# Reordering the border between the graph layers and the recurrence of a four-layer GNN kernel

## The chip, the cores and the metric

The kernel runs on one core of a Trainium2 chip. The metric is the device time of one execution in microseconds, as the median of several runs. The profile of one execution comes with it: its span, the instructions of each engine and the transfers. Engines are TensorE (PE; its weight loads are a row of their own, PEld), VectorE (DVE), ScalarE (ACT), GpSimd (POOL) and SyncE (SP), which here only issues transfers.

## The reference, cut to what matters

There are 16 graphs of 1024 nodes with 256 features. Each of four layers normalises x, applies relu, runs a graph operator and adds the result to x:

```
for layer in (attention, normalised adjacency, recurrence, MLP):
    h = relu(layernorm(x))
    x = x + layer(h, adj)
```

Layer 2 is the recurrence. With `dinv` the inverse row sums of `adj` (0 where a sum is 0), it goes through the nodes one after the other, and every node reads the states of its neighbours, new ones where they have been updated already:

```
norm_adjT = swapaxes(adj, 1, 2) * dinv[:, :, None]
for i in range(1024):                     # for all 16 graphs together
    x_par = norm_adjT[:, i] @ h           # sums over neighbours
    r, z  = split(x_i @ W_ioux.T + b_ioux + x_par @ W_iouh.T + b_iouh)
    r, z  = sigmoid(r), sigmoid(z)
    hc    = tanh(x_i @ W_coux.T + b_coux + (x_par * r) @ W_couh.T + b_couh)
    h[:, i] = z * x_par + (1 - z) * hc
```

## The kernel before, in words

**Layers 0 and 1** (`layers_0_1`) run as one loop over the graphs, i = 0 to 15. Matrix products with the adjacency are written as seven products of 512x512 quarters (`sums`, line 384), and the work of everything else is hung into seven hooks between these products: `a0` to `a6` in the first sums of an iteration (layer 0 of graph i), `d0` to `d6` in the second (layer 1 of graph i). In this part the order on all five engines, SyncE's queue included, is the order in which the Python code emits the instructions. `weights` (423) multiplies the sums by the layer's matrix; `Moments` (331) collects the layer norm's mean and variance, the squares on ScalarE; `normed` (361) applies relu((x - mean) * rs) on ScalarE, eight tiles of 128x256. The quarters lie in ten slots `at0` to `at9`.

**Jobs.** The recurrence wants its nodes in another order than the graph's (blocks of 128 nodes, inside a block 8 steps of 16, in an order that a side calculation finds on DVE). For every graph b a `Job` (497) brings what the recurrence reads into that order:

- `load` (513) gets `ad` (the adjacency near the diagonal, `near`, 1 MB), `ab` (the first block's columns, 0.5 MB) and, for b < 14, the normalised h, `h2`, from `he_d`. For 14 and 15 h2 stays where `normed` wrote it.
- `mask` (523) writes the permutation matrix `to` on DVE (L526) and zeroes triangles of `ad` and `ab` with affine selects on POOL (L529, L531); `scale` (534) multiplies `ad` by dinv on POOL, two instructions (L536, L537).
- `turn` (540) permutes and transposes h2 on TensorE (L547), evicts it (L550 ScalarE, L552 DVE) and stores it as `heT_d`.
- `first` (555) multiplies the first block's columns with h2 (L559), `base` (583) turns that into order and stores `base_d`.
- `order` (563) permutes `ad` (L570, L572), evicts it (L577 ScalarE, L579 DVE) and stores `near_d` and `next_d` (L580, L581).

Jobs 0 to 13 run two to an iteration, from i = 9 to 15, `run_a` in the first half and `run_b` in the second. Behind the loop stands a tail (from line 820): the rest of job 13, the last weights, and jobs 14 and 15 from their loads on.

**The border.** `layer_2` (866) begins with the weights `wx`, the biases, and small constants on DVE and POOL; then `load_he(0)` (1001) brings block 0 of `heT_d` for all graphs into `he`, in three parts (graphs 0 to 13, 14, 15); `Gates(he, 0)` (1040) copies the 16 columns of step 0 into `hs` on POOL (L1046) and multiplies them by `wx` on TensorE (L1056). `Sub(0, 0)` (1011) gathers 128 rows for each half of the graphs out of `near_d` into `aj` (L1020, indirect DMA on POOL) and spreads them into `ai` and `bd` on POOL (L1027, L1036). `bxt` is block 0's base, loaded from `base_d`; `wh` are the weights of the hidden state. In layer 2 the order on TensorE, DVE, ScalarE and POOL is that of the code; SyncE's queue is ordered by the scheduler, by when a load's slot is free.

**The recurrence** loops over 8 blocks t and 8 steps s. A step starts with x = bxt + near, runs `round_` (the gates of the hidden state, L1110), turns the new h and stores it; between its matmuls it works off a list of tasks: the gates of the next step, the far sums, and `base_tasks` (902), which compute the base of block t + 1 out of `ab` (columns) and `hb` (rows of he_d), one graph after another (L942). POOL masks each `ab` first (L920); ScalarE evicts each base sum (L929) ahead of the step's tanh. `last_tasks` (971) loads `ao` out of `next_d`, and `load_he(t + 1)` the next block's `he`. At the end of the recurrence layer 3 starts.

Of the kernel before, what the change touches and what calls it, by code (L numbers as in the profile page):

```python
# [16 lines left out]
P = 128  # L17
# [4 lines left out]
S = 16  # L22
# [20 lines left out]
def gnn_stack(ctx: ExitStack, tc: tile.TileContext, a: dict, out: bass.AP):  # L43
# [29 lines left out]
    dinv = const.tile([P, B, NT], F32, name="dinv")  # L73

# [194 lines left out]
    def layers_0_1():  # L269
        with ExitStack() as st:  # L270
# [226 lines left out]
            class Job:  # L497
# [24 lines left out]

                def mask(self):
                    b, ad, ab = self.b, self.ad, self.ab
                    self.to = to = self.tile("to", [P, NT, P])
                    nc.vector.tensor_tensor(to, step[:, None].to_broadcast([P, NT, P]),  # L526
                                            place.rearrange("i (t b) -> i t b", b=B)[:, :, b : b + 1].to_broadcast([P, NT, P]),
                                            ALU.is_equal)
                    nc.gpsimd.affine_select(out=ad[:, :, P:], in_=ad[:, :, P:], compare_op=ALU.is_gt, fill=0.0, base=0,  # L529
                                            pattern=[[0, NT], [-1, P]], channel_multiplier=1)  # L530
                    nc.gpsimd.affine_select(out=ab[:, 0], in_=ab[:, 0], compare_op=ALU.is_ge, fill=0.0, base=0,  # L531
                                            pattern=[[-1, P]], channel_multiplier=1)

                def scale(self):
                    b, ad = self.b, self.ad
                    nc.gpsimd.tensor_tensor(ad[:, :, P:], ad[:, :, P:], dinv[:, b][:, :, None].to_broadcast([P, NT, P]), ALU.mult)  # L536
                    nc.gpsimd.tensor_tensor(ad[:, 1:, :P], ad[:, 1:, :P],  # L537
                                            dinv[:, b, 1:][:, :, None].to_broadcast([P, NT - 1, P]), ALU.mult)

                def turn(self):  # L540
                    b, to = self.b, self.to
                    hT = big.tile([P, DC, N], F32, name=self.names.get("hT", "hT"))
                    for c in range(DC):
                        for t0 in range(0, NT, 4):
# [4 lines left out]
                            if t0 == 0 or not self.tail:  # L549
# [3 lines left out]
                    nc.gpsimd.dma_start(heT_d[b], hT)  # L553

                def first(self):
# [5 lines left out]
                    nc.scalar.activation(self.bs, pb[:, :D], AF.Copy, scale=dinv[:, b, 0:1])  # L561

                def order(self):
# [3 lines left out]
                    for t0 in range(0, NT, 2):  # L567
# [8 lines left out]
                        if t0 % 4 == 0:  # L576
                            nc.scalar.copy(got, pt)  # L577
                        else:
                            nc.vector.tensor_copy(got, pt)  # L579
                    nc.gpsimd.dma_start(near_d.rearrange("(t b j) n -> b j t n", t=NT, b=B)[b], ao[:, :, : P + S])  # L580
# [11 lines left out]
                def rest(self):  # L592
                    self.first()
                    self.order()
                    self.base()
# [49 lines left out]

            jobs = {i: (Job(2 * (i - 9)), Job(2 * (i - 9) + 1)) for i in range(9, 16)}
            jobs[15][1].names = {"ao": "h1"}
            job14 = Job(14, {"ad": "at7", "ab": "ds", "to": "at0", "hT": "q", "ao": "hT", "bs": "s1", "bo": "s2"})
            job15 = Job(15, {"hT": "h1", "ao": "q"})

            for i in range(B):
# [4 lines left out]
                def a0():  # L656
                    if ahead and i:
                        load_x(i + 1)
                    if run_a:
                        run_a.load()  # L660
                    side(1.0)
# [39 lines left out]
                def a6():  # L701
                    if ahead:
                        mean[i + 1].middle()
                        mean[i + 1].second(lo)
                    side(0.0 if run_a else 2.0)
# [40 lines left out]
                def d0():  # L746
                    if ahead:
                        plus(i + 1, "t1", "b11")
                        get(i + 1, "t3", 0, 1)
                    if m2:  # L750
# [8 lines left out]
                def d2():  # L759
# [4 lines left out]
                    if ahead:  # L764
                        add_f(i + 1, lo)
                    side(1.0)
# [6 lines left out]
                def d4():  # L773
# [5 lines left out]
                    if run_b:  # L779
                        run_b.mask()  # L780
                    side(0.5)
                def d5():
# [3 lines left out]
                    if run_b:  # L786
                        run_b.scale()
                def d6():
                    plus_row(x[i], "bias", 3)
                ags[i] = sums(i, left_of, [d0, d1, d2, d3, d4, d5, d6], lambda name: drop(i, name))  # L790
                if run_b and ahead:
                    run_b.turn()
                if m2:
                    m2.shift = small.tile([P, NT], F32, name="m_shift")
                    nc.vector.tensor_mul(m2.shift, m2.neg, m2.rs)
                if not ahead:
                    break
# [22 lines left out]
            h2[14] = big.tile([P, NT, D], F32, name="h2", bufs=2)  # L820
            normed(h2[14], x[14], m2.shift, m2.rs, all_)
            nc.sync.dma_start(rows(he_d[14]), h2[14])
            job14.load()
            m2 = Moments(x[15], "n", big.tile([P, 2, D], F32, name="s2").rearrange("p a d -> p (a d)")[:, :D])
            weights(x[15], ags[15], w1, dis[15], m2)
            nc.sync.dma_start(rows(x2_d[15]), x[15])
            m2.root()
            run_b.first()
            run_b.turn()
            shift = small.tile([P, NT], F32, name="shift")  # L830
            nc.vector.tensor_mul(shift, m2.neg, m2.rs)
            job14.mask()
            run_b.order()
            run_b.base()
            job14.scale()
            h2[15] = big.tile([P, NT, D], F32, name="h2", bufs=2)
            normed(h2[15], x[15], shift, m2.rs, all_)
            nc.sync.dma_start(rows(he_d[15]), h2[15])
            job15.load()
            job14.first()  # L840
            job14.turn()
            job14.base()
            job15.mask()
            job15.turn()
            job15.first()
            job15.base()
            job15.scale()
            job14.order()
# [17 lines left out]
    def layer_2(shared, early):  # L866
        with ExitStack() as st:
            wp = st.enter_context(tc.tile_pool(name="w2", bufs=1, reuse_waits="tile"))
# [7 lines left out]
            load_w(wx, "W_iouxT", "W_couxT")  # L876

            bias = wp.tile([P, 3, DC], F32, name="bias")
            bias2 = wp.tile([P, 3, DC], F32, name="bias2")
            with nc.allow_non_contiguous_dma(reason="biases, once"):  # L880
                for t, io, co in ((bias, "b_ioux", "b_coux"), (bias2, "b_iouh", "b_couh")):
                    nc.sync.dma_start(t[:, :2].rearrange("p q c -> p (q c)"), a[io].rearrange("(k p) -> p k", p=P))
                    nc.sync.dma_start(t[:, 2], a[co].rearrange("(c p) -> p c", p=P))
            nc.vector.tensor_add(bias, bias, bias2)
# [17 lines left out]
            def base_tasks(t, bxt):  # L902
# [4 lines left out]
                def load(b):  # L907
                    ab = big.tile([P, NT, P], F32, name="ab")
                    nc.sync.dma_start(ab, a["columns"][b, t])
                    hb = shared.tile([P, NT, D], F32, name="hb")  # L910
# [60 lines left out]
            def last_tasks(t, bxt):  # L971
# [4 lines left out]
                def load(b0):  # L976
                    ao = big.tile([P, 4, n], F32, name="ao", bufs=4)
                    nc.sync.dma_start(ao, next_d[b0 : b0 + 4, t - 1].rearrange("b p i -> p b i"))
# [20 lines left out]
            parts = ((0, B - 2), (B - 2, B - 1), (B - 1, B))  # L999

            def load_he(t):
                he = big.tile([P, DC, B, P], F32, name="he")
                for b0, b1 in parts if t == 0 else ((0, B),):
                    for c in range(DC):
                        nc.sync.dma_start(he[:, c, b0:b1], heT_d[b0:b1, :, c, t * P : (t + 1) * P].rearrange("b p i -> p b i"))
# [203 lines left out]
            with tc.manual_schedule(engines={mybir.EngineType.PE, mybir.EngineType.DVE, mybir.EngineType.Activation, mybir.EngineType.Pool}):  # L1209
                he = load_he(0)  # L1210
                gx = Gates(he, 0)
                sub = Sub(0, 0)
                bxt = shared.tile([P, DC, B, P], F32, name="bxt")
                for b0, b1 in parts:
                    for c in range(DC):
                        nc.sync.dma_start(bxt[:, c, b0:b1], base_d[b0:b1, :, c].rearrange("b p i -> p b i"))
                load_w(wh, "W_iouhT", "W_couhT")
# [9 lines left out]
                near = gx_ahead = None  # L1227
                behind = []
                for t in range(NT):
                    if t == NT - 1:  # L1230
                        eye = next(early)
                    base_todo = None
                    if t + 1 < NT:
# [6 lines left out]
                    for s in range(NS):  # L1240
# [15 lines left out]
                        else:  # L1256
                            if s == 1 and t + 1 < NT:
                                he_next = load_he(t + 1)
                            if s == 1 and t > 0:
# [555 lines left out]
```

## Time and profile before

| | before |
|---|---|
| median of 3 runs | 4196.85 us (4190.28 to 4197.19) |
| the profiled execution: time, span | 4196.59 us, 4194.7 us |
| TensorE busy, share, instructions | 4010.6 us, 96%, 19307 |
| DVE, ACT, POOL busy | 2578.6, 1631.5, 1643.9 us |
| DMA moved, mean rate | 744.71 MB, 178 GB/s |
| mean granted clock of TensorE | 0.985 |

The profiled execution took 1.9 us more than its span. The span divides roughly into layers 0 and 1 (to 1281 us, the last product of iteration 15), the border (to 1360.6, the first L1110), the recurrence (to about 2940) and layer 3. Views of the trace used below: stretches (busy time of each engine, granted clock and DMA share in a given window), the timeline of an engine (instructions in order of time, with the idle time before them and what ended it), and lists of transfers with their time from issue to landing. Times are counted from the span's start.

### The profile page before, as it was taken

To read this page: it belongs to the slowest core of one execution; us is meant where nothing else is said; L and a number is where in the kernel's file an instruction comes from. 1 tells how busy PE (TensorE), PEld (TensorE's weight loads), DVE (VectorE), ACT (ScalarE), POOL (GpSimd) and SP (SyncE) were. 2 spreads that over 40 slices of the span, in tenths; PEclk is the share of its full clock that TensorE was granted. 3 is DMA by queue.
4 is the path that set the end of the run, shared out by engine and by line. 5 is a ranking of instruction groups with operands and counts; after the bars stand their busy time and mean duration, and the time that the engine had idled before them with its cause. 6 is when DMAs were issued, how large, how long until landed. Compare 5 with 4: busy or idle time off the path is not lost. (4 is left out here: it accounts for less than half of the span.)

```text
span 4194.7 us, 56476 instructions
## 1 busy us (share of the span) xinstructions
PE 4010.6 (96%) x19307; PEld 2798.4 (67%) x19307; DVE 2578.6 (61%) x6015; ACT 1631.5 (39%) x4172; POOL 1643.9 (39%) x1740
## 2 busy tenths in 40 slices
PE   7999999999897999999999999998899999999998
PEld 3545455555565888888888888877465665656656
DVE  7888865677742444444444444454677877777776
ACT  3565656545453232322223232333333344333332
POOL 2232323434334324333333333332555364463552
PEclk9999999999998999999999999998999999999999
DMA  6676669888768354646454645431634434334320
GB/s 239 213 231 231 223 203 258 295 283 313 254 213 271 128 188 154 193 131 201 138 189 151 196 144 181 141 125 39 235 111 141 150 121 161 121 130 171 112 100 21
DMA packets 406701, 744.71 MB, mean 178 GB/s; under 512 B 75168, under 2 KB 325664, under 8 KB 365344
## 3 DMA queue, kind: packets, MB, share of 16 engines
q1 hardware_dynamic: 370976, 613.49, 42.6%
q0 software_dynamic: 26080, 109.21, 9.1%
q10 hardware_dynamic: 9216, 16.78, 1.2%
q8 instruction: 209, 3.42, 0.3%
q14 instruction: 220, 1.80, 0.1%
HBM read 538.85 MB, written 183.76 MB: 172 GB/s over the span
## 5 line engine op out<-in xcount | busy, mean ns | idle before, releaser
L86 POOL TENSOR_TENSOR rs<-rs_v,mhalf 128x8 f32<-128x8 f32 (+1 forms) x65 | 112.1, 1725 | 920.6 <-DVE rs_v L82 461.5
L942 PE MATMUL pf<-hb,ab 128*128 128x256 f32 x1568 | 415.4, 383 | 0.3 <-DMA hb<-he_d 0.3
L1056 PE MATMUL pf<-hs,wx 128*128 128x256 f32 x1536 | 348.9, 383 | 12.3 <-POOL hs L1046 12.1
L1056 PEld LDWEIGHTS pf<-hs,wx 128*128 128x128 f32 x1536 | 292.5, 192 | 54.8 <-POOL hs L1046 13.4
L1599 POOL TENSOR_TENSOR ss<-ss,sq 128x512 f32<-128x512 f32 x224 | 299.3, 1351 | 22.8 <-ACT sq L1597 16.7
L1369 POOL DMA_INDIRECT hs_d<-h,table x128 | 129.0, 1008 | 444.8 <-ACT gates L1064 366.8
L942 PEld LDWEIGHTS pf<-hb,ab 128*128 128x128 f32 x1568 | 272.0, 191 | 37.9 <-issue 7.4
L1061 DVE TENSOR_TENSOR gates<-pf,bias 128x512 f32<-128x512 f32 x128 | 88.4, 691 | 282.6 <-PE pf L1056 282.6
L1662 PEld LDWEIGHTS po<-w,hh 128*128 128x128 f32 x2048 | 238.1, 193 | 16.6 <-issue 11.0
L428 PE MATMUL pmm<-w,ag 128*128 128x256 f32 x1024 | 232.6, 386 | 13.2 <-DVE ag L419 8.1
L1662 PE MATMUL po<-w,hh 128*128 128x128 f32 x2048 | 242.3, 277 | 1.4 <-ACT hh L1645 0.7
L428 PEld LDWEIGHTS pmm<-w,ag 128*128 128x128 f32 x1024 | 196.4, 193 | 52.0 <-DVE ag L419 10.2
L1597 ACT ACTIVATE sq<-hh 128x512 f32<-128x512 f32 x224 | 141.3, 631 | 199.5 <-POOL ss L1599 122.7
L1545 PE MATMUL ph<-bxt,hb 128*128 128x512 f32 x440 | 200.3, 601 | 14.0 <-ACT hb L1517 11.0
L1154 ACT ACTIVATE r<-pr 128x128 f32<-128x128 f32 (+2 forms) x256 | 57.8, 278 | 349.7 <-PE pr L1110 344.9
L1092 PE MATMUL pf<-bd,h 128*128 128x384 f32 (+4 forms) x512 | 182.8, 449 | 1.4 <-DVE bxt L1095 1.4
L1095 DVE TENSOR_TENSOR bxt<-bxt,pf 128x384 f32<-128x384 f32 (+4 forms) x256 | 127.4, 500 | 82.4 <-PE pf L1092 79.9
L1595 DVE SCALAR_TENSOR_TENSOR hh<-ph,b,u 128x512 f32<-128x512 f32 x192 | 141.1, 748 | 43.9 <-PE ph L1591 34.1
L1645 ACT ACTIVATE hh<-hh,rw 128x512 f32<-128x512 f32 x256 | 158.7, 708 | 23.8 <-DVE hh L1644 23.8
L1545 PEld LDWEIGHTS ph<-bxt,hb 128*128 128x128 f32 x440 | 82.8, 193 | 112.0 <-issue 92.5
L350 ACT ACTIVATE pt<-x,m_neg 128x256 f32<-128x256 f32 x240 | 114.3, 476 | 108.7 <-DVE m_neg L345 102.4
L1644 DVE TENSOR_TENSOR hh<-hh,po 128x512 f32<-128x512 f32 x256 | 154.3, 673 | 2.9 <-PE po L1641 2.9
(377 smaller groups left out, 9200.3 us busy)
## 6 DMA issues: line engine op xcount, KB each, us to landing
at<-in_quarters SPq DMA_DIRECT2D x94, 1024.0 KB, 9.6
t_d<-at SPq DMA_DIRECT2D x64, 1024.0 KB, 10.2
ab<-in_columns SPq DMA_DIRECT2D x127, 512.0 KB, 6.9
bxt<-t_d SPq DMA_DIRECT2D x42, 1024.0 KB, 5.5
bxt<-in_quarters SPq DMA_DIRECT2D x34, 1024.0 KB, 5.1
at<-at POOLq DMA_DIRECT2D x30, 1024.0 KB, 8.8
at<-t_d SPq DMA_DIRECT2D x22, 1024.0 KB, 4.8
pc<-in_own ACTq DMA_DIRECT2D x64, 256.0 KB, 7.3
```

What stands on the lines that cost most here:

```text
L428: nc.tensor.matmul(po[:, t - t0], ag[:, c, t * P : (t + 1) * P], w[:, c], start=c == 0, stop=c == DC - 1)
L942: nc.tensor.matmul(pb, ab[:, jts[k]], hb[:, jts[k]], start=k == 0, stop=k == len(jts) - 1)
L1056: nc.tensor.matmul(pg[:, e], wx[:, c, q * D + e * P : q * D + (e + 1) * P], self.hs[:, c], start=c == 0, stop=c == DC - 1)
L1092: nc.tensor.matmul(pf, h[:, g, c * P : (c + 1) * P], bd[:, g, b0 : b0 + n, S : S + far], start=True, stop=True)
L1369: nc.gpsimd.indirect_dma_start(out=hs_d[t][g][:, :], out_offset=row(1, g, t, s), in_=h[:, g], in_offset=None)
L1545: nc.tensor.matmul(pa, st[left][:, k], at[q % 6][:, k], start=onto is None and k == 0, stop=k == 3, skip_group_check=True)
L1595: behind3[:] = [nc.vector.scalar_tensor_tensor(hh[q][:, k], ph, b1[:, k : k + 1], u, op0=ALU.add, op1=ALU.add)]
L1597: nc.scalar.activation(sq, hh[q][:, k], AF.Square)
L1599: nc.gpsimd.tensor_tensor(ss[q], ss[q], sq, ALU.add)
L1644: nc.vector.tensor_mul(hh[q][:, k], hh[q][:, k], pr)
L1645: nc.scalar.activation(hh[q][:, k], hh[q][:, k], AF.Silu, scale=rw[:, k : k + 1])
L1662: nc.tensor.matmul(po[:, n], left[:, c, n * P : (n + 1) * P], right[:, c], start=onto is None and n == 0 and c == 0, stop=c == HH - 1, ski ...
```

## The change

The jobs 14 and 15 are taken apart. Their `near` loads are issued in the first sums of iteration 15 (hook a0) into slots `at7` and `at8`, their columns in the second sums (d0) into `at0`; masks and permutations are made in a6 to d6; their `scale` becomes 15 instructions of 128x128 on ScalarE for each job, in hooks d4 and d5. h2 of graph 14 is normed and stored in d6. In the tail, job 14's `order` comes first, then the last weights, job 13's first, turn and base, h2 of graph 15, job 14's turn, first and base, job 15's turn and first, job 13's order, job 15's base and order. Job 14's evictions are all on DVE. Job 15 stores the first block of `heT_d` by itself. The stores of x2 and he_d for the last graphs go from SyncE's queue to POOL's.

In layer 2 the biases are loaded and added at the kernel's start. `wx` and `wh` are asked for together; `he` and `bxt` are loaded alternately in four parts (graphs 0 to 12, 13, 14, 15); the first `hb` has a slot of its own at the start of its pool. `Gates(he, 1)` is made ahead of `Sub(0, 0)`, so both `hs` copies stand ahead of the gathers on POOL. For block 1, `he` is loaded at step 3 and `ao` at step 4; a one-column memset on POOL holds each of these loads there (for `he`, its first half).

```diff
 class Job:
+    def near(self, name):
+        self.ad = big.tile([P, NT, 2 * P], F32, name=name)
+        nc.sync.dma_start(self.ad, a["near"][self.b])
+    def columns(self, ab):
+        self.ab = ab
+        nc.sync.dma_start(ab, a["columns"][self.b, 0])
...
     def scale(self):
         b, ad = self.b, self.ad
+        if b > 13:
+            for t in range(NT):
+                nc.scalar.activation(ad[:, t, P:], ad[:, t, P:], AF.Copy, scale=dinv[:, b, t : t + 1])
+                if t:
+                    nc.scalar.activation(ad[:, t, :P], ad[:, t, :P], AF.Copy, scale=dinv[:, b, t : t + 1])
+            return
         nc.gpsimd.tensor_tensor(ad[:, :, P:], ad[:, :, P:], dinv[:, b][:, :, None].to_broadcast([P, NT, P]), ALU.mult)
...
     def turn(self):
-        nc.gpsimd.dma_start(heT_d[b], hT)
+        if b < 15:
+            nc.gpsimd.dma_start(heT_d[b], hT)
+        else:
+            nc.gpsimd.dma_start(heT_d[b, :, :, :P], hT[:, :, :P])
+            nc.gpsimd.dma_start(heT_d[b, :, :, P:], hT[:, :, P:])
...
+            with nc.allow_non_contiguous_dma(reason="biases, once"):
+                for t, io, co in ((bias, "b_ioux", "b_coux"), (bias2, "b_iouh", "b_couh")):
+                    nc.sync.dma_start(t[:, :2].rearrange("p q c -> p (q c)"), a[io].rearrange("(k p) -> p k", p=P))
+                    nc.sync.dma_start(t[:, 2], a[co].rearrange("(c p) -> p c", p=P))
+            nc.vector.tensor_add(bias, bias, bias2)
...
                 def a0():
+                    if not ahead:
+                        job14.near("at7")
+                        job15.near("at8")
...
                 def d0():
+                    else:
+                        ab = big.tile([P, 2, NT, P], F32, name="at0")
+                        job14.columns(ab[:, 0])
+                        job15.columns(ab[:, 1])
+                        job15.mask_near()
...
-            h2[14] = big.tile([P, NT, D], F32, name="h2", bufs=2)
-            normed(h2[14], x[14], m2.shift, m2.rs, all_)
-            nc.sync.dma_start(rows(he_d[14]), h2[14])
-            job14.load()
+            job14.order()
             m2 = Moments(x[15], "n", big.tile([P, 2, D], F32, name="s2").rearrange("p a d -> p (a d)")[:, :D])
             weights(x[15], ags[15], w1, dis[15], m2)
-            nc.sync.dma_start(rows(x2_d[15]), x[15])
             m2.root()
+            nc.gpsimd.dma_start(rows(x2_d[15]), x[15])
+            shift = small.tile([P, NT], F32, name="shift")
+            nc.vector.tensor_mul(shift, m2.neg, m2.rs)
             run_b.first()
             run_b.turn()
-            shift = small.tile([P, NT], F32, name="shift")
-            nc.vector.tensor_mul(shift, m2.neg, m2.rs)
-            job14.mask()
-            run_b.order()
             run_b.base()
-            job14.scale()
             h2[15] = big.tile([P, NT, D], F32, name="h2", bufs=2)
             normed(h2[15], x[15], shift, m2.rs, all_)
-            nc.sync.dma_start(rows(he_d[15]), h2[15])
-            job15.load()
+            job14.turn()
             job14.first()
-            job14.turn()
             job14.base()
-            job15.mask()
+            nc.gpsimd.dma_start(rows(he_d[15]), h2[15])
             job15.turn()
             job15.first()
+            run_b.order()
             job15.base()
-            job15.scale()
-            job14.order()
+            run_b.keep_order()
             job15.order()
...
+                load_part(he, 0, 0, 13)
+                load_base(0, 13)
+                load_part(he, 0, 13, 14)
+                load_base(13, 14)
...
                 gx = Gates(he, 0)
+                gx_ahead = Gates(he, 1)
                 sub = Sub(0, 0)
...
-                            if s == 1 and t + 1 < NT:
+                            if s == (1 if t else 3) and t + 1 < NT:
                                 he_next = load_he(t + 1)
+                            if s == 4 and t + 1 < NT:
+                                aos = load_next(t + 1)
```

## The prediction

> **What bounds it now.** I read the page first. TensorE is busy 96% of the span, but slice 13 of 40 (1258 to 1363 us) is one of its few 7s, and the DMA digit there is 8. So I opened that border in stretches: one between the last product of iteration 15 (1281) and the first matmul of the recurrence (1360.6).
>
> ```profile
> 1281.00:1288.00 7.00, 7.00 (x34) 6.17 (x33) 5.33 (x17) 4.80 (x11) 3.33 (x3) 1.00 0.01 2
> 1288.00:1316.60 28.60, 17.16 (x99) 13.54 (x98) 9.54 (x19) 13.25 (x32) 12.24 (x14) 0.86 1.02 355
> 1316.60:1336.40 19.80, 12.93 (x49) 9.38 (x49) 3.98 (x8) 2.82 (x5) 9.32 (x13) 0.76 1.10 302
> 1336.40:1360.60 24.20, 15.89 (x47) 11.83 (x48) 3.17 (x8) 2.88 (x6) 10.18 (x13) 0.73 1.10 332
> ```
>
> Columns: stretch, length, busy PE, weight load, DVE, ACT, POOL; granted clock, DMA share, GB/s. In 79.6 us TensorE works 53.0 and stands 26.6, at a clock down to 0.73. The transfers are at their limit from 1288 on, yet at 0.01 just before. The timeline of TensorE then says who ended each stop (start, length, what, [idle before <- by whom]):
>
> ```profile
> 1307.18 1.06 PE L547 MATMUL pt<-to,h 128*128 128x128 f32 x8 [2.11 <-DVE to L526]
> 1316.62 6.55 PE L559 MATMUL pt<-h,ab 128*128 128x256 f32 x16 [6.12 <-POOL ab L531]
> 1336.39 6.94 PE L1056 MATMUL pf<-hs,wx 128*128 128x256 f32 x24 [3.82 <-POOL hs L1046]
> 1354.22 6.52 PE L1056 MATMUL pf<-hs,wx 128*128 128x256 f32 x16 [8.31 <-POOL hs L1046]
> 1360.58 1.89 PE L1110 MATMUL pr<-x,wh 128*128 128x256 f32 x8
> ```
>
> and those of SyncE's queue and POOL, why POOL was late:
>
> ```profile
> 1301.62 1.37 SPq L516 DMA_DIRECT2D ad<-in_near  x1
> 1303.05 1.26 SPq L518 DMA_DIRECT2D ab<-in_columns  x1
> ```
>
> ```profile
> 1312.76 1.09 POOL L529 TENSOR_SCALAR_AFFINE_SELECT ad<-ad 128x1024 f32<-128x1024 f32 x1 [5.51 <-DMA ad<-in_near]
> 1316.28 0.29 POOL L531 TENSOR_SCALAR_AFFINE_SELECT ab<-ab 128x128 f32<-128x128 f32 x1 [2.43 <-DMA ab<-in_columns]
> 1333.79 0.92 POOL L580 DMA_DIRECT2D near_d<-q  x1 [2.32 <-DVE own L887]
> 1343.21 1.09 POOL L1020 DMA_INDIRECT aj<-near_d,table  x1 [6.46 <-DMA next_d<-q]
> 1349.26 3.75 POOL L1036 TENSOR_TENSOR bd<-aj,own 128x1024 f32<-128x1024 f32 x2 [3.67 <-DMA aj<-near_d,table]
> 1353.77 0.73 POOL L1046 COPY hs<-he 128x256 f32<-128x256 f32 x2
> ```
>
> Job 15's inputs are asked for at 1301.6, into full DMA, and land 11 to 13 us later (6.12). The second `hs` copy, 0.73 us of work, stands in POOL's queue behind two gathers that wait for the last stores of the border (8.31). Two blocks of matmuls after long stops run at about 0.41 us each: L559, 6.55 us against 3.62 at 1287.84, and 16 L1056, 6.52 against 16 x 0.215 = 3.44 at full clock. Together 6.0 us of cold clock.
>
> **The change, part by part**, along TensorE's new order, from 1281.0, with the durations above.
>
> Before 1281: 2 MB of `near` start at about 1213 (DMA 0.82 busy at 1200 to 1220, 0.56 after) and are not needed before 1270; 1 MB of columns follow at 1260. POOL's two extra affine selects (1.1 us each) fall into its idle 8.8 and 11.5 us, DVE's two `places` (1.22) into its idle 8.9. If that cover were gone they would cost 1 to 2.5 us.
>
> Scale on ScalarE: 30 instructions of 128x128, SBUF to SBUF, a form the trace lacks. L363 does 128x256 in 4.04/8 = 0.505 us each; half the columns can't take more, and not under half (0.25). I take 0.30, near the 0.277 of the 128x128 `z` from PSUM: 9.0 us from 1274.8 (ACT waits 8.3 us there now), so job 14 is ready at 1279.3, before TensorE wants it, and job 15 at 1283.8. Then h2[14] (4.04) to 1287.8, the squares of the moments, now paced by the later weights, to 1294.5, and h2[15], behind two `hT` evictions, 1297.8 to 1301.8 (1301.1 now). At 0.505 ACT ends the scales at 1290 and turning job 13 waits for its evictions: +4.5 us. At 0.25, nothing won.
>
> [...]
>
> TensorE: job 14's order comes first. Four packs, each evicted by DVE (0.61) behind L419 and m_shift (1.39 next to a busy POOL): 3.9 us, to 1284.9. Weights 7.07 as now, to 1292.0; job 13's first 3.5 and turn, with its two stops, 2.7: 1298.2; job 14's turn 2.8 and first with base 4.5 (3.6 plus a DVE eviction between): 1305.5; job 15's turn 2.8, first 3.6: 1311.9. No stop: its columns are masked since 1285, h2[15] is there since 1301.8. Job 13's order with base 3.6, job 15's order 3.2: 1318.7. DVE evicts until 1319.2.
>
> POOL issues near and next of job 15 (0.95 each) and the mask of `before` until 1321.5, then `hs`. That needs job 15's `he`. Its 128 KB are stored alone, from 1307.5; 8.3 MB stand in the queues from 1288 (near, next, he_d of job 14, x2, two heT, he_d of 15, the first bxt), which at 330 GB/s (302 to 355 in the rows above) are through by 1313; with 2 us to land, the load goes at 1315 and lands 5 us later, 1320, before POOL is free. TensorE stops 3.2 us and starts at 1321.9 (3.82 now). 24 gates, cold as now, 6.9: 1328.8; three seeds 2.6: 1331.4; the 16 gates of the next step at once, warm, 3.5, since both `hs` copies now stand ahead of the gathers: 1334.9. DVE's copy of `bxt` needs job 15's base: stored 1316.5, landed 1321.6, loaded by 1327 to 1331, copied by 1332. So L1110 starts at 1334.9 and not 1360.6: **25.7 us earlier**. Cross-check: of the 26.6 idle and 6.0 cold about 7 remain (3.2, and 3 to 4 on DVE evictions).
>
> [...] I keep the row: 24 matmuls after 3.82 us took 0.287 each, between cold and warm.
>
> What is late next: 7.7 us after L1110 TensorE takes the base sums L942, and tanh on ACT stands behind their eviction. They need POOL's masks L920, behind the gathers. Near of job 15 leaves at 1319.3; by 1333.79 to 1343.21 (9.4) the gathers go at 1328.7, land 6.0 later, bd 3.75, ai 0.9, two more gathers 2.4, masks 0.6: 1342.3 against 1342.6. Now there are 10.8 us to spare, then none: every us by which near lands later costs one. ab and hb load from 1323, due 1342.
>
> Moved into the recurrence: he of block 1 (one half; the other stays early, behind the stores) and four ao, 2 MB, at steps 3 and 4; DMA is 0.27 to 0.5 busy from 1380 to 1480, so nothing; if base loads were held up, 6 us for 2 MB at 330 GB/s. The five memsets on POOL take 0.1 each. At the start four bias loads are put into SyncE's queue behind x(1), and DVE's add waits for them with the whole DVE queue behind it, at 34.6. In the border they landed within 21 us at full DMA (issued 1307 to 1316, added 1337); from 22 that is 43, less 4 us before TensorE needs DVE: 0 to 5 us. I take 0, as DMA is free there and the row is an upper end. One queue now carries all stores (POOL), but 1296 to 1304 it moved 1.9 MB in 8 us beside others.
>
> **Sum.** 4196.6 of the profiled execution (span 4194.7 and 1.9 around it), less 25.7: 4170.9; the median of the runs, 4196.85, is 0.3 above it. I say 4171. Main case: 31 us won if the stop, cold gates and half of the new evictions vanish (4166); 16 if ACT takes 0.505 and the bias 5 (4181).
>
> **Rivals.** (1) The border stays bound by transfers: at 268 GB/s, the mean of 1280 to 1380, the 8.3 MB are through at 1319; landing 2, issue 0.5 and the slow 8.0 of the small he loads give 1329.5 and L1110 at 1343: 4179; with near landing as late as well, 5 more, up to 4186. For it: DMA share 1.1; against: 5 MB of loads leave this stretch, and DMA stands idle at 1281. (2) Nothing is won: the recurrence waits for something that did not move. It would have to be the gathers, if near landed 25 us later than I say; the slowest store of the border took 9.8. 4197. (3) Slower: ACT becomes the bound. All 30 scales stand ahead of h2[14], the moments and h2[15]; each 1 us per instruction costs 30. With some 3 us of slack and 25.7 won, it turns from 1.25 us per instruction and passes +0.2% at 1.54 (at 1.6: 4207). Against: the wider L363 takes 0.505.
>
> **Numbers.** Main 0.72, rival 1 0.16, rival 2 0.05, rival 3 0.07. 0.2% (8.4 us) is about what a measurement of this kernel can tell from no change. Faster 0.88, within 0.05, slower 0.07. The range takes the main case with 2 us more at its low end, and rival 1 up to 4186.
>
> **What would show it.** After: L1110's first block near 1335; no 6 us stop before job 15's first; the 16 gates at 3.5 us directly behind the seeds; near 30 new ACT rows of 0.3 us; 2 MB less in the border. Wrong if TensorE waits there for `he` or masks by over 6 us, if ACT rows exceed 0.5, or if DVE stands at 34.6 for the bias.

## The result, and the profile after

| | before | after |
|---|---|---|
| median of 5 runs | 4192.46 us (4190.19 to 4197.19) | 4178.31 us (4171.42 to 4179.26) |
| the profiled execution: time, span | 4196.59, 4194.7 us | 4179.26, 4177.5 us |
| last product of iteration 15 done, next matmul starts, at | 1280.9 us | 1284.8 us |
| border: from there to the first hidden-state matmul | 79.65 us | 56.86 us |
| from the first hidden-state matmul to the last matmul of the kernel | 2825.8 us | 2827.8 us |

The ratio after/before is 0.9963, 95% interval 0.9952 to 0.9973: 15.5 us less (11 to 20). The prediction said 25.7 us. The border alone became 22.8 us shorter; TensorE reached it 3.85 us later, and 2.0 us went after it (22.8 - 3.85 - 2.0 = 16.9; the span lost 17.2). Below, "the border" is always the distance in the fourth row, "warm" and "cold" mean full and half granted clock (1.00 and 0.50), the "seeds" are the six matmuls that start `pr`, `pz` and `pc` ahead of the hidden state, and line numbers are those of the kernel whose profile is shown.

The same three stretches as before, cut at the places that correspond (stretch, length, busy PE, weight load, DVE, ACT, POOL; granted clock, DMA share, GB/s):

```profile
1284.80:1292.00 7.20, 5.36 (x25) 4.23 (x24) 4.38 (x6) 6.66 (x18) 4.14 (x6) 0.77 0.89 229
1292.00:1323.80 31.80, 28.32 (x157) 22.36 (x155) 13.48 (x38) 14.33 (x34) 11.51 (x17) 1.00 0.89 316
1323.80:1341.60 17.80, 13.97 (x46) 10.76 (x47) 6.47 (x11) 3.03 (x7) 8.78 (x13) 0.81 1.00 307
```

The middle stretch now runs at full clock with 3.5 us of standing still; transfers no longer wait until 1288 to begin (0.89 in the first row). What is left lies at the two ends, where the clock is 0.77 and 0.81. The timeline of TensorE:

```profile
1287.66 0.33 PE L606 MATMUL pt<-at,at 128*128 128x128 f32 x1 [1.84 <-DVE q L615]
...
1288.64 8.76 PE L431 MATMUL pmm<-w,ag 128*128 128x256 f32 x32
...
1314.45 3.67 PE L592 MATMUL pt<-h,at 128*128 128x256 f32 x16
...
1327.63 8.14 PE L1134 MATMUL pf<-hs,wx 128*128 128x256 f32 x24 [3.88 <-POOL hs L1124]
...
1338.19 3.62 PE L1134 MATMUL pf<-hs,wx 128*128 128x256 f32 x16
1341.64 1.89 PE L1188 MATMUL pr<-x,wh 128*128 128x256 f32 x8
```

Job 15's first (L592) follows its turn without a stop, warm, where 6.12 us of waiting and 6.55 of cold work stood. The 16 gates of the next step follow the seeds directly, warm, where 8.31 us of waiting stood. One stop in front of the first gates is left, ended by POOL's copy of `hs`. The last weights take 8.6 us until the next instruction, not 7.07. On ScalarE the new rows follow each other every 0.293 us (0.39 long, overlapping):

```profile
1280.67 0.39 ACT L560 ACTIVATE at<-at,dinv 128x128 f32<-128x128 f32 x1
1280.96 0.39 ACT L562 ACTIVATE at<-at,dinv 128x128 f32<-128x128 f32 x1
```

### The profile page after: what moved, and what is told of

Same layout as the page of the kernel before. It is cut to its first block, busy times and chain, and to the rows that moved or that the text cites. A ratio compares the mean times of both kernels' runs of the same rounds, so it can differ in the third digit from the quotient of the medians.

```text
span 4177.5 us, 56510 instructions
## 1 busy us (share of the span) xinstructions
PE 4008.7 (96%) x19307; PEld 2797.5 (67%) x19307; DVE 2586.1 (62%) x6021; ACT 1644.1 (39%) x4197; POOL 1642.1 (39%) x1745
```

## The experiments

Each ratio is to the kernel before in the same comparison. Theory: the border is a chain of separate waits, which can be taken away one by one; what is missing in the gain are terms that the sum sized wrongly. Rival: the transfers bind it, and each wait removed comes back as another.

**1. Early loads alone**, in the kernel before (job 15 only):

```diff
                     if run_a:
                         run_a.load()
+                    if not ahead:
+                        job15.ad = big.tile([P, NT, 2 * P], F32, name="at8")
+                        nc.sync.dma_start(job15.ad, a["near"][15])
...
+                    else:
+                        job15.ab = big.tile([P, 2, NT, P], F32, name="at0")[:, 0]
+                        nc.sync.dma_start(job15.ab, a["columns"][15, 0])
...
-            job15.load()
```

> The kernel before, with one part of the change alone: job 15's near and columns are loaded in the first and second sums of iteration 15; every other order stays. Theory 1 (the border is a chain of separate waits, as the prediction summed it): the stop of 6.12 us before job 15's first goes, and its cold clock with it (6.55 us against 3.62 warm), so the first L1110 block comes 6.1 + 2.9 = 9.0 us earlier and the kernel takes about 9 us less than before (ratio 0.998). Theory 2 (the border is bound by its transfers, DMA share 1.0 to 1.1): the wait only moves to the loads of he and to the gathers, and the gain is 0 to 3 us. In the profile, theory 1 wants the distance from the last product of iteration 15 to the first hidden-state matmul at 70.6 us (79.65 before), theory 2 at 77 or more.

Ratio 0.9981 (0.9972 to 0.9990), 8 us; border 70.32 us, 9.33 less. TensorE:

```profile
1303.80 3.69 PE L559 MATMUL pt<-h,at 128*128 128x256 f32 x16
...
1322.39 7.72 PE L1061 MATMUL pf<-hs,wx 128*128 128x256 f32 x24 [5.49 <-POOL hs L1051]
...
1339.01 6.22 PE L1061 MATMUL pf<-hs,wx 128*128 128x256 f32 x16 [6.32 <-POOL hs L1051]
```

The wait before job 15's first is gone and the block is warm (3.69 us for 16, 6.55 before); the first gates wait 1.7 us longer than before (5.49 against 3.82). Theory 1 holds: 9.0 was expected. The total is met in part by luck, though: the first gates came 7.8 us earlier, and the other 1.5 us were won behind them, mostly in the second stop (6.32 us against 8.31), which this edit was not meant to touch.

**2. Gates ahead alone**, in the kernel before:

```diff
                 gx = Gates(he, 0)
+                gx_ahead = Gates(he, 1)
                 sub = Sub(0, 0)
```

> The kernel before, with another part alone: the gates of step 1 are made ahead of the gathers of step 0, so both pairs of hs copies stand ahead of the gathers in POOL's queue. Theory 1 (separate waits): the stop of 8.31 us and the cold clock of the 16 gates (6.52 against 3.44 us) go, 11.4 us in all; the gathers, issued 0.73 us later, are hidden by the 10.8 us which the masks have to spare. Distance from the last product to the first hidden-state matmul 68 to 69 us (79.65 before), kernel 11 us below before (ratio 0.9973). Theory 2 (transfers): x = bxt, or the masks behind the gathers, end the next wait, and no more than 5 us are won.

Ratio 0.9974 (0.9963 to 0.9984), 11 us; border 66.90. Of the 12.75 us, 9.87 lie between the first gates and the first hidden-state matmul (24.19 before, 14.32 now) and belong to the edit:

```profile
1333.42 8.45 PE L1056 MATMUL pf<-hs,wx 128*128 128x256 f32 x24 [3.82 <-POOL hs L1046]
...
1344.28 3.62 PE L1056 MATMUL pf<-hs,wx 128*128 128x256 f32 x16
```

The first gates themselves came 2.9 us earlier, which this edit does not touch. The traces show where: job 15's columns landed 0.3 us earlier, its 16 first products took 5.11 us instead of 6.55 (0.32 us each, between 0.215 warm and 0.41 cold), and its order 1.1 us less. 3.6 us are given back at once: the second step starts 24.6 us after the first one, not 21.0. Of these, 1.9 are a wait of the second base sum for its `hb`; the rest, 1.7, is half of 3.41 us, what one window of half clock would cost (an estimate from the clock's steps in the changed kernel's profile).

**3. Both at once.**

> The kernel before with both small parts at once: job 15's near and columns loaded early, and the gates of step 1 ahead of the gathers. Alone they shortened the border from 79.65 to 70.32 and to 66.90 us. Theory 1 (separate waits, they add): 79.65 - 9.33 - 12.75 = 57.6 us, close to the 56.7 to 56.9 of the whole change, so that the other parts (scales on ScalarE, job 14's order first, loads in four parts, biases at the start) are worth about 1 us together; of it some 3 us are given back in the first step, whose gathers and masks come late, as in the run of the gates alone (first to second step 24.6 us instead of 21.0). Kernel 17 to 20 us below before. Rival: the other parts carry several us, since the transfers that they moved out of the border hold the loads of he and the gathers: 61 us or more.

Ratio 0.9969 (0.9957 to 0.9981), 13 us; border 60.28. The expectation of 57.6 missed by 2.7, since it counted the 2.9 us of experiment 2 that its edit does not touch: 79.65 - 9.33 - 9.87 = 60.45. So the two parts do add, by a reckoning that was made after the result. But 5.0 us are given back in the first step (26.0): POOL's `bd` is late and VectorE's product r runs beside it (2.13 us for its two halves, 0.76 in the kernel before); and the second base sum waits for its `hb` (second line):

```profile
1343.39 2.16 PE L1115 MATMUL pc<-r,wh 128*128 128x256 f32 x8 [1.65 <-DVE r L1160]
...
1361.65 0.67 PE L947 MATMUL pf<-hb,ab 128*128 128x256 f32 x2 [3.21 <-DMA hb<-he_d]
```

The whole change has a border of 56.86 and a first step of 21.0. So its other parts (loads in four parts, `wx` and `wh` early, the first `hb` in a slot of its own, the order of the jobs) are worth 3.4 us in the border and 5.0 behind it, and not about 1 us as I had expected. The kernel's time shows little of it (0.9963 against 0.9969), because the biases at the start cost some 6 us elsewhere (experiment 10).

**4. The scales back on POOL**, in the changed kernel:

```diff
-                    if b > 13:
+                    if b > 15:
```

> The changed kernel with the scales of jobs 14 and 15 back on POOL (two instructions each, 3.56 us per job), in the same two hooks. Theory 1: ScalarE's part of the change carries weight, because POOL is occupied there from 1279.6 to 1288.7: job 14's scale ends at 1287.0 instead of 1283.0, its order waits 2.3 us more, the last bias row of x comes at 1295.3 instead of 1288.2 and holds up the first evictions of the weights by some 2 us, and small DVE work beside POOL takes longer: 3 to 6 us slower than the changed kernel. Rival: POOL's idle time hides all of it and ScalarE gets 8.8 us back for h2 of graphs 14 and 15: no difference, or 1 us faster. In the profile: distance from the last product to the first hidden-state matmul 60 to 63 us under theory 1, 56 to 57 under the rival (56.9 in the changed kernel).

Ratio 0.9949 (0.9935 to 0.9962); border 57.40, 0.5 us longer. My theory of 3 to 6 us fell: ScalarE's part is worth next to nothing, and the kernel does not take longer with the scales on POOL (0.9949 against 0.9961 and 0.9963; the intervals overlap). Job 14's order waited for POOL (0.44 and 1.31 us) where it had waited for VectorE's evictions (1.84), and took 4.8 us against 3.9; the weights behind it took 8.3 against 8.6, and the late bias row held up none of their products.

**5. Job 14's order woven into the last weights**, in the changed kernel:

```diff
-            job14.order()
+            packs = job14.packs()          # order(), one pack of transposes a time
...
-            weights(x[15], ags[15], w1, dis[15], m2)
+            for t0 in range(0, NT, 2):
+                weights(x[15], ags[15], w1, dis[15], m2, pairs=(t0,))
+                next(packs)
```

> The changed kernel with job 14's order woven into the last weights: after each of the four pairs of weight products one pack of four (three) transposes, so that VectorE's evictions run beside TensorE's work. Theory 1 (the missing part of the gain is in TensorE's own chain: stops on evictions and the halved clock behind them): the order costs 1.65 us instead of 3.9, the weights run at full clock (7.1 instead of 8.6 us), and the border is 3.0 to 3.8 us shorter, 53 to 54 us instead of 56.9. Theory 2 (the transfers set the end: job 15's part of h lands at 1324.3 in the changed kernel, 3 us before POOL is free for it): TensorE only waits longer before the first gates, 0 to 1 us shorter. The first matmul of the gates tells them apart: 39 us after the last product under theory 1, 42 to 43 under theory 2 (42.85 in the changed kernel).

Ratio 0.9944 (0.9930 to 0.9957); border 53.34, 3.5 us less, the first gates at 39.38 us after the last product. Theory 1 holds, and transfers follow: job 15's part of h came earlier with the rest of the chain. Weights and order take 8.55 us together, at a clock of 1.00. The ratio is 7 to 8 us below that of the changed kernel; the border accounts for 3.5 of them, the rest is within what the runs vary.

**6. The changed kernel once more.**

> The changed kernel once more, unchanged. Up to the last product of iteration 15 it issues the same work as the kernel before, yet its profile came there 3.85 us later (most of it at one place, iteration 11's first weights, where small VectorE instructions ran beside a POOL scale). Theory 1: these 3.85 us are chance, from when a transfer lands; the last product will lie anywhere between 1274 and 1286, as in the profiles so far (1274.3 to 1285.3), while the border stays at 56.9 us within 0.3. Theory 2: the early part of the change (loads of near at the start of iteration 15, biases at the start) costs it, and it lies at 1284 to 1285 again. Under both the median is 16 to 19 us below the kernel before.

Ratio 0.9961 (0.9948 to 0.9975); border 56.69; last product at 1283.1. That tells neither theory from the other; experiment 10 does.

**7. The seeds ahead of the first gates**, in the changed kernel: the loop over (pr, pz, pc) stands before `for task in gx.tasks`.

> The changed kernel with one block moved: the six matmuls that seed pr, pz and pc (2.6 us, they need wx and no h) stand ahead of the first 24 gates instead of behind them, in TensorE's stop of 3.88 us. Theory 1 (the terms mis-sized in the sum are the stop and the halved clock behind it): the stop shrinks to 1.3 us, the 24 gates run warm for the larger part (5.2 to 6.9 us instead of 8.1), the first hidden-state matmul comes 3.5 to 5.5 us earlier; up to 3 us of it are lost again at the first base sum, whose mask ends at 1347.2 in the changed kernel with 2.1 us to spare. Net 2 to 4 us below the changed kernel. Rival: x = bxt on VectorE or the last part of bxt sets the first hidden-state matmul (the copies end 0.06 us before it in the changed kernel), and it comes no more than 1 us earlier.

Ratio 0.9955 (0.9942 to 0.9969); border 52.39. The stop shrank to 1.31 us, the 24 gates took 5.45 us, all warm (clock 1.00 from 1326.40 to 1331.80). The first step then gave 3.0 us back (24.0): r beside `bd` took 3.01 us for two instead of 0.76, and the first base sum stood 0.60 us for its mask. The net gain is 1.3 to 1.5 us by these two distances against the two profiles of the changed kernel, and 2.5 to 3.4 us by the ratios, whose intervals overlap; 2 to 4 were expected.

```profile
1339.60 3.01 DVE L1233 TENSOR_TENSOR r<-r,x 128x256 f32<-128x256 f32 x2 [2.78 <-ACT r L1232]
```

**8. The first `hs` copies on VectorE**, in the changed kernel: `Gates(he, 0, nc.vector)`, `Gates(he, 1, nc.vector)`, with `before`, `change` and `hT` made behind them.

> The changed kernel with the four first hs copies on VectorE instead of POOL, ahead of the mask and the constants that VectorE made there. It tells whether POOL's queue or job 15's part of h ends TensorE's stop of 3.88 us. If POOL's queue does (five stores, 4.7 us, in front of the copies), the first gates start 2 to 2.7 us earlier, at 40.2 to 40.9 us after the last product (42.85 in the changed kernel), part of the cold clock may go too, and the kernel takes 2 to 3 us less. If the landing of he sets it, the start stays within 0.5 us and nothing is won.

The first gates came at 40.06, border 52.06: POOL's queue, not the landing, ended the stop. But the first step took 26.2 us, 5.2 more, and the ratio is 0.9965 (0.9953 to 0.9977): nothing won, where 2 to 3 us were expected. Here a border that ends earlier than POOL's `bd` allows only moved the wait: r runs beside `bd` (2.98 us, 0.76 in the kernel before), and behind TensorE's stops on r (1.05 and 1.34 us) the next 14 matmuls take 3.1 us more than warm ones, about what two windows of half clock cost (an estimate, 1.7 us each).

```profile
1336.25 2.98 DVE L1228 TENSOR_TENSOR r<-r,x 128x256 f32<-128x256 f32 x2 [2.78 <-ACT r L1227]
```

```profile
1339.28 2.93 PE L1183 MATMUL pc<-r,wh 128*128 128x256 f32 x6 [1.34 <-DVE r L1228]
1342.00 3.61 PE L1129 MATMUL pf<-hs,wx 128*128 128x256 f32 x8
```

**9. One store of job 15's heT**, in the changed kernel: `nc.gpsimd.dma_start(heT_d[b], hT)` for all jobs.

> The changed kernel with job 15's heT written by one store of 1 MB again instead of 128 KB and 896 KB. The 128 KB landed 4.6 us after issue and the he load followed at 1319.2; the 896 KB landed at 1321.7. With one store the load of he goes at about 1321.5 and lands at 1326.5, while POOL is free for the copies at 1326.5 (one issue of 0.68 us less). Theory 1: hidden, no difference within 0.5 us (the small store has a cover of 3 us by POOL's queue). Rival: the prediction's step that the early landing carries the gain; then the first gates start 2 to 3 us later.

Border 56.67, first gates at 42.77, ratio 0.9965 (0.9951 to 0.9978): the store by itself wins nothing as long as POOL's queue stands in front of the copies.

**10. The biases at the kernel's start**, in the kernel before: two tiles in the constants' pool, four loads behind x(1), one add; the loads and the add of the border are taken out.

> The kernel before, with the biases loaded and added at the kernel's start. In the seven profiles with the change so far iteration 11's weights come 93.7 to 97.0 us before the next iteration's, in the three without 91.0 to 92.4, and the last layer-1 weights before iteration 15 lie at 1233.1 to 1239.3 against 1228.3 to 1234.4. The biases are the only part of the change that touches anything before iteration 15. Theory 1 (chance): the distance stays at 91 to 93 and the kernel takes the time of before within 3 us. Theory 2 (the shifted transfers or the moved tiles cost 2 to 4 us there): 93.7 to 97, and the kernel is 2 to 4 us slower than before. The border stays at 79.6 within 1 us under both.

Ratio 1.0014 (1.0004 to 1.0023): 6 us slower (2 to 10). Theory 2 holds by the time. The distance from iteration 11's weights to the next iteration's is 96.7 us, the border 79.52. The distance alone does not tell the theories apart: the kernel of experiment 3, without the early biases, has 94.2, inside the range that was put down to them. Nothing waits at the start (the add took 0.16 us at 34.3 in the changed kernel). This one profile reaches the border 1.0 us later than before and ends 3.3 us later; over all profiles, the last layer-1 weights before iteration 15 come at 1228.3 to 1234.4 us (mean of four 1232.1) without the early biases and at 1233.1 to 1241.5 (mean of ten 1236.6) with them, 4.5 us. It is plainest at iteration 11, but that is not the whole of it: 2.8 of the 4.5 us lie between the means at that iteration's first weights already, where one profile without the early biases is over 5 us ahead of the other three. Kernel before:

```profile
954.03 0.26 DVE L111 TENSOR_SCALAR pc<-pc 128x192 f32<-128x192 f32 x1 [0.54 <-DMA pc<-in_own]
...
956.79 3.29 PE L428 MATMUL pmm<-w,ag 128*128 128x256 f32 x14 [0.60 <-DVE ag L416]
```

and with the biases at the start (VectorE, POOL, TensorE):

```profile
953.45 0.26 DVE L113 TENSOR_SCALAR pc<-pc 128x192 f32<-128x192 f32 x1 [1.15 <-DMA pc<-in_own]
...
955.18 1.90 DVE L212 SCALAR_TENSOR_TENSOR pc<-o_sub,pc 128x46 f32<-128x46 f32 x1
957.11 1.60 DVE L213 SCALAR_TENSOR_TENSOR o_bins<-pc,o_bins 128x46 f32<-128x46 f32 x1
958.64 0.68 DVE L418 TENSOR_TENSOR ag<-ag,py 128x512 f32<-128x512 f32 x1
```

```profile
955.12 1.89 POOL L538 TENSOR_TENSOR ad<-ad,dinv 128x1024 f32<-128x1024 f32 x1
```

```profile
959.37 7.82 PE L430 MATMUL pmm<-w,ag 128*128 128x256 f32 x23 [4.36 <-DVE ag L418]
```

Against the work in front of it, the side calculation's load lands 0.6 us later. Its small instructions, 0.27 us each otherwise, then fall beside POOL's mask and scale; three of four take 1.2 to 1.9, and the add that TensorE needs stands behind them. In all ten profiles with the early biases the wait for `pc` is 1.15 to 1.32 us and TensorE's stop 4.36 or 4.37; in the four without it is 0.54 to 0.63, and the stop comes in two parts, 0.6 and 1.86. A possible reason for the later landing shows in the DMA queues. From 100 to 1230 us (packets, MB, share of 16 engines), first the kernel before, then with the biases at the start:

```profile
q1 hardware_dynamic: 113515, 211.17, 51.4%
```

```profile
q1 hardware_dynamic: 113328, 210.44, 52.3%
```

Fewer bytes take more time. By size, the packets of 1024 bytes in this part took 49.7 to 49.9 ns on average in the four kernels without the early biases and 52.6 to 53.0 in the ten with them, 6% more; in the recurrence both groups lie at 50.2 to 51.0. That the early biases make these packets slower is shown by this split. That the slower packets are what delays the load at iteration 11 is argued, not shown.

Why they are slower is open. By the code, the two bias tiles, 24 bytes of each partition each, are made ahead of the tiles of layers 0 and 1, which should then lie further along in each partition; no profile shows the addresses. The single packets are not all slower by the same amount: the median is 46 ns in the kernel before and with the biases at the start, but 85% took 46 or 47 ns before and 52% with the biases, and the 95% quantile went from 69 to 79. No run moved the tiles back, so their place is a possible cause and not a shown one.

**11. A faster version**: experiments 5 and 7 together, and POOL's last stores in the order near of 13, near of 15, next of 13, next of 15.

> A version meant to be faster: the changed kernel with job 14's order woven into the last weights, the seed matmuls ahead of the first gates, and POOL's last stores in the order near of 13, near of 15, next of 13, next of 15. Worked out from the runs: gates at 39.4 us after the last product, 24 gates 5.5, a gap of 0.6, 16 gates 3.5: first hidden-state matmul at 49.0 us (56.9 in the changed kernel). The gathers go 1 us earlier by the order of the stores, so bd leaves POOL at about 52.3, before VectorE multiplies r (52.5), and the masks end at 56.1, before the first base sum at 56.7: nothing given back, 7 to 8 us below the changed kernel, ratio to before 0.994. If the mask or bd is late all the same, 3 us of it are lost in the first step, as in the run with the seeds alone.

Ratio 0.9944 (0.9930 to 0.9958), median 4169.75 us; border 50.72 and a first step of 21.0: nothing given back, since `bd` and masks now come early enough (r takes 0.76 us).

```profile
1328.25 10.59 PE L1150 MATMUL pf<-hs,wx 128*128 128x256 f32 x40 [2.21 <-POOL hs L1140]
1338.67 1.89 PE L1204 MATMUL pr<-x,wh 128*128 128x256 f32 x8
```

Expected were 49.0; the first gates came 0.9 us later than in experiment 5 (40.30), and the mean clock of the border is 0.97, as one window of 3.41 us at 0.50 gives (an estimate).

**12. The same with the `hs` copies on VectorE.**

> The version before this one in the list, and the first hs copies on VectorE. The gates can start about 1.5 us earlier (POOL's mask and copies no longer stand in front, but job 15's part of h lands only about 37 us after the last product): first hidden-state matmul at 47 to 48 us. Its r then meets bd on POOL and the masks end at 56 us against a need at 55.3: 1 to 2.5 us given back in the first step. Net 0 to 1 us against the version before it; a loss of up to 1 us is as likely as a gain, since in the run with these copies alone 5 of 4.8 us were given back (first to second step 26.2 us instead of 21.0).

Border 46.99, clock 1.00 from the seeds to the first hidden-state matmul (1318.9 to 1330.6), first step 24.0: 3.0 given back (r takes 2.99 us beside `bd`), ratio 0.9946 (0.9932 to 0.9960). Versions 5, 11 and 12 are alike in time, some 7 us (0.17%) below the changed kernel by the ratios (0.9944 to 0.9946 against 0.9961 and 0.9963); their intervals touch that of the changed kernel.

## Why the prediction was right, and where not

The direction, the place and the two main mechanisms were right; three terms were mis-sized, all to the same side. That the time still lies in the main case (4166 to 4181) is in part luck: its slow end was made of 4.5 us on ScalarE, which did not come, and 5 on the biases, which came by another way; the weights and the first gates took the place of the former.

- *Job 15's loads early* (6.12 + 2.93 us): 9.33 in experiment 1. Right in kind; 7.8 of it came ahead of the first gates and 1.5 behind them.
- *Second stop and its cold gates* (8.31 + 3.1): 9.87 in experiment 2. Right in kind, 1.5 too large, because the first 24 gates got slower (8.3 us to the seeds, 6.8 before). In the kernel before one window of half clock lies in them (1336.03 to 1339.44, 0.50); 8.3 is about what two would give, an estimate from 24 x 0.215 = 5.2 warm and 1.7 for each window.
- *Job 14's order 3.9 us*: 3.86. Right; but the weights behind it were taken at full clock, 7.07. They took 8.60, with the clock at 0.50 from 1288.75 to 1292.16: the first mis-sized term, 1.5 us. Experiment 5 won it back together with the eviction stops.
- *Stop 3.2 and gates 6.9*: 3.88 and 7.98, together 1.8 us more; here two windows of half clock (1326.30 to 1333.12, 0.50) stand in place of the one in the row that was carried over. POOL's stores, not the landing of job 15's `he` (1324.3, predicted 1320 on a clock 3.85 us earlier, so 0.5 us off), ended the stop: as said, and shown by experiments 8 and 9. The profile before does not show the 2 us which that step (and rival 1) took for a store to land: in it the stores of 128 KB took 4.6 to 10.2 us from issue, in the changed kernel job 15's part of `heT` took 4.6 and two base stores 2.2 each; the load of `he` went at 1319.2 (predicted 1315, again on a clock 3.85 us earlier). With the weights this makes 3.3 us; the border missed by 2.9.
- *Scales on ScalarE at 0.30 us*: 0.293. The price was right and did not matter: on POOL they cost 0.5 us of border (experiment 4). ScalarE's idle time was worth looking at; POOL's should have been put beside it.
- *Masks without slack*: 2.1 us to spare in the changed kernel, where the sum had 0.3. With a shorter border the masks and POOL's `bd` beside r were the next bound: experiments 7 and 12 lost 3 us there, experiment 8 lost 5, with the 3.1 us of slower matmuls that followed. Experiments 2 and 3 lost 3.6 and 5.0 in the first step mainly on the wait for `hb` (1.9 and 3.2 us).
- *Bias at the start, 0 of 0 to 5 us*: the step that failed. I priced only the wait of the add at 34.6, and looked for it there. That wait is nothing. The cost came hundreds of microseconds later: TensorE reached the border 3.85 us later in the profile, and experiment 10 puts the biases at 6 us (2 to 10). Slower packets go with it; by which way they cost TensorE time, and why they are slower, is not settled. The place was wrong as well as the size.
- *Moved loads of the recurrence, 0*: the first step is 21.0 us in both kernels. The 2.0 us lost behind the border are not settled. The distance to the last matmul was 2824.7 to 2831.1 us in the profiles that gave nothing back in the first step, one of 2828.5 without these moved loads, so 2.0 us is within what it varies. Luck has a part in all of these sums: job 15's first products (1.4 us) and order (1.1), which its edit does not touch, moved the border of experiment 2 by some 2.5 us.
- *Rival 1* (transfers bind the border, first hidden-state matmul at 1343 or later on before's clock, a border of 62 us or more): refuted by experiments 5, 7, 8, 11 and 12, which brought the border from 56.9 to as little as 47.0 with the same transfers. *Rival 3* (ScalarE the bound) is refuted by 0.293 us.

On the clock: in the border of the changed kernel the granted clock is 0.50 for 3.41 us (1288.75 to 1292.16) and for 6.83 us (1326.30 to 1333.12), and 1.00 elsewhere. The same profile in windows of 3.41 us along these steps (columns as above):

```profile
1285.34:1288.75 3.41, 1.57 (x13) 1.15 (x12) 3.26 (x5) 3.41 (x11) 3.36 (x4) 1.00 1.19 302
1288.75:1292.16 3.41, 3.41 (x10) 2.70 (x9) 0.76 (x2) 2.71 (x6) 0.40 (x1) 0.50 0.52 127
...
1319.47:1322.88 3.41, 2.62 (x19) 1.77 (x18) 1.92 (x4) 1.17 (x2) 0.69 (x2) 1.00 0.63 242
1322.88:1326.30 3.42, 0.87 (x7) 0.51 (x5) 1.52 (x5) 0.59 (x1) 3.12 (x5) 1.00 0.68 217
1326.30:1329.71 3.41, 2.08 (x5) 1.72 (x6) 0.95 (x2) 0.00 (x0) 2.37 (x6) 0.50 0.99 216
```

No window is idle. One that was busy for 1.57 of 3.41 us (46%) is followed by half clock, and so is one with 0.87 (25%); one with 2.62 (77%) is not. Over the 14 profiles, from 1180 to 1400 us cut into such windows along the clock's own steps, all 798 windows at full clock with 52% of work or more were followed by full clock, and 29 of the 31 with 51% or less by half clock; elsewhere in the kernel the edge is less sharp. So here the clock of a window goes with the share of work in the window before it, and the stop of 1.84 us on an eviction in job 14's order was enough: the weights behind it took 8.60 us, not 7.07.

## What to carry to other kernels

Price an edit by everything that it touches: two tiny tiles, loaded and added at the start where nothing waited for them, cost this kernel 6 us (2 to 10), as much as a good stop in the border gains. After taking a wait away, look at what the next engine still has to do at the new time: here 3 of the 4.4 us won by the seeds were given back to POOL's `bd` and masks, and none any more when job 14's order was woven in and the stores in front of the gathers were put in another order as well (experiment 11). And a stop can be filled with work that needs nothing from what it waits for: the seeds cut TensorE's stop from 3.88 to 1.31 us, and the 24 gates behind it ran at a clock of 1.00 in 5.45 us instead of 8.14.

## What the runs showed of the hardware that was not expected

- Granted clock: 0.50 for the 3.41 us after a window in which TensorE had 46% of work, with no stop longer than 1.84 us in it.
- Small VectorE instructions with two tensor operands beside POOL's masks and products: 0.27 us alone, 1.03 to 1.90 beside one; r of two halves 0.76 us alone and 2.13 to 3.01 beside `bd`. The slowest of the small ones (1.90 us, biases at the start) ends at 957.08 us, POOL's product beside it at 957.01. A small instruction with one tensor operand was slowed as well: 128x8 took 1.57 us beside such a product (kernel before, at 956.66) and 0.16 alone.
- Packets of 1024 bytes in layers 0 and 1: 49.7 to 49.9 ns on average without the two bias tiles in the constants' pool, 52.6 to 53.0 with them; 85% of the packets at 46 or 47 ns, or 51 to 52%.
